# Two hypernetwork convolution layers: first weights by ScalarE, statistics merged in two steps, a normalization stage on VectorE, W2 and the hidden vectors loaded in other pieces

## The chip, the cores and the metric

The kernel runs on one core of a Trainium2 chip. A core has TensorE (matmuls and, beside them, weight loads), VectorE, ScalarE, GpSimd and SyncE; in the profile they are PE and PEld, DVE, ACT, POOL and SP. All transfers of this kernel are issued by SyncE, in program order. The metric is the device time of one execution in microseconds, and before and after are compared by the median of several executions.

## The reference

Two layers of the same form run one after the other on x, shaped (s, b, c, l) = (32, 32, 64, 256), float32. Each layer normalizes x by groups over l (32 groups of 8 positions; mean and variance over everything of one sample s that lies in the group: all b, all c, 8 l), convolves the result along l with weights that differ for every (b, l), adds a bias, and adds the input x back.

```python
h = jax.nn.relu(_ln(z @ W1 + b1, g1, be1))            # hidden vector of each (b, l)
w = (h @ W2 + b2).reshape(B, L, CI, CO, K)            # its own 64x64x3 weights
hb = jax.nn.relu(_ln(z @ Wb1 + bb1, gb1, beb1))
bias = (hb @ Wb2 + bb2).transpose(0, 2, 1)
xp = jnp.pad(x, ((0, 0), (0, 0), (0, 0), (pad, pad)))
x_uf = jnp.stack([xp[..., i:i + L] for i in range(K)], axis=-1)
out = jnp.einsum('sbilk,bliok->sbol', x_uf, w) + bias[None]
# layer: x = x + conv(_gn(x), ...)
```

The statistics of a layer need all of its x, so no product of a layer can start before the last piece of its input exists. The weights of a layer do not depend on x.

## The kernel before, in words

**Units.** u counts batches over both layers (64 in all; u = 32, written B, begins the second layer). v counts half-batches, 32 output channels each; v = 64, written NH * B, begins the second layer. For one v, TensorE makes the weights of all positions in 12 groups (`order`: 4 blocks of 8 output channels times 3 kinds), each one PSUM tile `pg` made from the hidden vector `hs[u]` and a piece of `w2` (lines 502 and 503, `make`). `take` adds b2 and puts the group into the SBUF tile `wall`: by VectorE for the kinds 0 and 1 and one half of kind 2 (line 514), by ScalarE for the other half of kind 2 (line 525), or wholly by ScalarE in eight or sixteen instructions if `scalar` is set. `products(v)` (line 548) then multiplies the normalized x in `xn` with `wall` in four groups of positions q, in two PSUM tiles `pc`; VectorE adds each group to the residual tile (line 558) and, in the first layer, takes its statistics (line 257).

**First phase** (`first_phase`). The whole of x is loaded in 16 blocks of 4 MiB (SyncE line 273, `load(q)`) into three places in turn, the last block into `xn`; block q + 3 is asked for after block q's statistics. VectorE takes the statistics of each block as it lands, into `first_parts`. Between them, spread evenly, runs the work on the hidden vectors of all 64 batches (class `Hidden`): z is loaded, TensorE, ScalarE, GpSimd and VectorE compute, and the hidden vectors and biases are stored to `hd` and `bd` in DRAM, one entry of `hd` for two batches. Also in SyncE's queue: four quarters of the first layer's W2 after the blocks 4 to 7, the hidden vectors of batches 0 and 1 after block 10 (line 124), and after block 14 batch 0's x (line 129) and two residuals (line 138). `first_weights` stands in front of block 14's statistics: GpSimd clears two strips of `wall`, and 9 of the first 12 weight groups are made and taken by ScalarE.

**From the statistics to the first product.** `batches` merges the parts of all batches into mean and variance (eight VectorE instructions, lines 368 to 375). `diagonals` takes the root on ScalarE and the reciprocal on VectorE, and lays mean and reciprocal root on diagonals: `gmean` by eight ScalarE instructions (402), `rstd` by one of VectorE (405). `spread` multiplies both with a matrix of ones on TensorE (419), so that every partition has them, and ScalarE copies them back (420). Then the last three weight groups are made and taken by VectorE, and VectorE normalizes batch 0 (`normalize_first`, 489) in three stages, each of four pieces with one subtraction and one multiplication. Meanwhile GpSimd adds the bias to the first residual (438).

**The train.** For every later v TensorE makes the first weight group of v, does the products of v - 1, and makes the other eleven. `after(v - 1)` stores the result, loads the residual of v + 1, the hidden vector of the next but one batch (when h = 1), stores pieces for the second layer (452), normalizes the next batch's half on GpSimd (`next_pairs`, 471, which then asks for the half of the batch after it, 131 in the second layer), and adds the next bias on GpSimd.

**Boundary.** After v = 63 there are statistics that only then are complete. The parts of all batches but the last were merged earlier (`batches(parts, B - 1)`); `last_batch` (382 to 392) merges the last in, `diagonals` follows, and after the fourth weight group of v = 64 `spread` and `normalize_first(B, nc.gpsimd)`, whose three stages run on GpSimd, then the loads of batch 33 and its normalization. A group q of products needs only some of the groups of positions: q = 0 is served by the first stage, q = 1 by the second as well, q = 2 and 3 by the third too.

The order on every engine and in SyncE's queue is the order of the program; nothing is rearranged.

## Time and profile before

| what | us |
|---|---|
| median of 9 runs | 4059.24 |
| lowest and highest of them | 4053.94, 4065.47 |
| the profiled execution's own time | 4065.47 |
| its span in the profile | 4063.5 |
| chain of work that ended last: TensorE's share | 87% |
| weights, PE lines 502 and 503, busy each | 2739.9, 2738.7 |
| products, PE line 548, busy | 976.7 |
| evictions of weights: DVE line 514, ACT line 525 | 1855.0, 1188.1 |

The profiled execution is the slowest of the nine. An "xN" behind an operation is a count; "<-" in brackets names what ended the idle time before an instruction. Matmuls overlap, so their busy times add up to more than the span. In the forty slices of the profile, TensorE is busy for six tenths and fewer in the first three slices (about 100 us each) and for nine tenths or more from then on; the granted TensorE clock stands at five to eight tenths in part of the first three slices and at nine tenths or more after them. The transfers move 334 and 335 GB/s in the first two slices, about half of that later.

### The profile page before, as it was taken

What the parts mean: (1) busy time and instruction counts of PE and PEld (TensorE: products, weight loads), DVE (VectorE), ACT (ScalarE), POOL (GpSimd) and SP (SyncE); (2) the same over time, 40 slices, a digit from 0 to 9 for tenths busy, and PEclk for the clock granted to TensorE, in tenths of its full rate; (3) what the DMA queues carried; (4) which work ended last, traced back from release to release, by engine and by line L of the source; (5) the groups of instructions that cost most, each with busy time, mean ns of one, the idle gap of its engine ahead of it and who ended that gap; (6) DMA issues with size and microseconds to landing.
All of it is one profiled execution on the core that took longest, in us unless ns stands there. A gap on an engine that the chain in (4) does not pass through costs nothing.

```text
span 4063.5 us, 194865 instructions
## 1 busy us (share of the span) xinstructions
PE 3867.3 (95%) x91064; PEld 3713.9 (91%) x91064; DVE 2601.7 (64%) x2934; ACT 1333.3 (33%) x4480; POOL 1944.5 (48%) x639
## 2 busy tenths in 40 slices
PE   6659999999999999999999999999999999999999
PEld 3349999999999999999988999999999999999998
DVE  7666666666666666666675556565656565656565
ACT  6542323333232323323222323232323233323232
POOL 5425553454345435534533645544554455445541
PEclk8579999999999999999999999999999999999999
DMA  8977777777777777777676545444544454445442
GB/s 334 335 259 194 198 171 188 184 184 186 181 190 176 190 171 187 185 180 187 166 193 178 171 139 171 130 161 139 171 130 161 142 168 140 159 146 156 141 147 88
DMA packets 655426, 718.59 MB, mean 177 GB/s; under 512 B 567380, under 2 KB 585112, under 8 KB 586136
## 3 DMA queue, kind: packets, MB, share of 16 engines
q1 hardware_dynamic: 654616, 706.13, 61.2%
q8 instruction: 711, 11.65, 1.2%
q14 instruction: 99, 0.81, 0.1%
HBM read 492.12 MB, written 213.91 MB: 174 GB/s over the span
## 4 chain that ended last, share of the span: by engine, by line
PE 87%; DVE 5%; DMA 3%; issue 2%; POOL 2%; ACT 1%; SPq 0%; DVEq 0%; POOLq 0%; ACTq 0%
PE pg L502 50%; PE pc L548 23%; PE pg L503 12%; DVE wall L514 2%; DVE parts L257 1%; DMA zt<-in_L_conv_z_dram 1%; DMA wall<-in_xs_dram 1%; DVE room L558 1%; PE p L185 1%; POOL xn L200 1%; POOL xn L489 1%; PE p L217 0%; DMA hd<-xn 0%; POOL xn L471 0%; DMA room<-in_xs_dram 0%
## 5 line engine op out<-in xcount | busy, mean ns | idle before, releaser
L502 PE MATMUL pg<-hT,w2t 128*64 128x128 f32 x24576 | 2739.9, 274 | 30.8 <-DVE wall L514 11.5
L503 PE MATMUL pg<-hT,w2t 128*64 128x128 f32 x24576 | 2738.7, 274 | 4.0 <-issue 3.4
L502 PEld LDWEIGHTS pg<-hT,w2t 128*64 128x64 f32 x24576 | 2685.6, 137 | 57.6 <-DVE wall L514 23.2
L503 PEld LDWEIGHTS pg<-hT,w2t 128*64 128x64 f32 x24576 | 2686.2, 137 | 9.0 <-issue 8.3
L514 DVE TENSOR_TENSOR wall<-pg,b 64x1024 f32<-64x1024 f32 x1527 | 1855.0, 1220 | 688.1 <-PE pg L503 684.7
L525 ACT ACTIVATE wall<-pg,b 64x128 f32<-64x128 f32 x4168 | 1188.1, 478 | 2605.3 <-DVE wall L514 2156.4
L471 POOL TENSOR_TENSOR xn<-room,gmean 128x2048 f32<-128x2048 f32 x124 | 572.6, 4618 | 1765.2 <-PE pc L548 1736.9
L548 PE MATMUL pc<-wall,xn 128*32 128x128 f32 (+2 forms) x40960 | 976.7, 253 | 59.3 <-issue 45.8
L548 PEld LDWEIGHTS pc<-wall,xn 128*32 128x32 f32 x40960 | 933.6, 111 | 106.8 <-issue 91.2
L558 DVE TENSOR_TENSOR room<-pc,room 128x512 f32<-128x512 f32 x512 | 353.9, 691 | 667.5 <-PE pc L548 601.8
L471 POOL TENSOR_TENSOR xn<-xn,rstd 128x2048 f32<-128x2048 f32 x124 | 655.3, 5285 | 9.7
L438 POOL TENSOR_TENSOR room<-room,bt 128x2048 f32<-128x2048 f32 x128 | 587.5, 4590 | 121.0 <-DMA bt<-bd 58.8
L257 DVE BATCH_NORM_STATS2 parts<-room 128x6 f32<-128x256 f32 (+1 forms) x592 | 241.7, 453 | 16.2 <-DMA room<-in_xs_dram 7.4
L200 POOL TENSOR_TENSOR xn<-xn 128x512 f32<-128x512 f32 (+2 forms) x192 | 103.8, 541 | 103.7 <-ACT xn L192 91.2
L257 DVE BATCH_NORM_STATS2 parts<-wall 128x6 f32<-128x512 f32 x160 | 97.6, 678 | 27.0 <-DMA wall<-in_xs_dram 27.0
L217 PEld LDWEIGHTS p<-ident,xn 128*128 128x128 f32 x256 | 45.4, 201 | 74.0 <-issue 62.1
L217 PE MATMUL p<-ident,xn 128*128 128x128 f32 x256 | 62.0, 410 | 44.4 <-DVE xn L209 39.7
L185 PE MATMUL p<-wc,zt 17*64 17x256 f32 x512 | 59.5, 602 | 28.2 <-DMA zt<-in_L_conv_z_dram 20.6
L185 PEld LDWEIGHTS p<-wc,zt 17*64 17x64 f32 x512 | 27.4, 206 | 59.4 <-issue 33.9
L219 ACT ACTIVATE xn<-p,vec 128x512 f32<-128x512 f32 x64 | 46.3, 773 | 21.3 <-PE p L217 21.3
L192 ACT ACTIVATE xn<-p 128x1024 f32<-128x1024 f32 x32 | 32.6, 1019 | 41.0 <-PE p L185 41.0
L213 ACT ACTIVATE xn<-p,var 128x128 f32<-128x128 f32 x128 | 36.4, 372 | 10.4 <-DVE xn L209 10.4
(59 smaller groups left out, 207.9 us busy)
## 6 DMA issues: line engine op xcount, KB each, us to landing
bt<-bd SPq DMA_DIRECT2D x512, 256.0 KB, 6.4
room<-in_xp_dram SPq DMA_DIRECT2D x64, 1024.0 KB, 9.7
room<-in_xs_dram SPq DMA_DIRECT2D x64, 1024.0 KB, 8.6
x<-room SPq DMA_DIRECT2D x64, 1024.0 KB, 5.3
x1p<-room SPq DMA_DIRECT2D x512, 128.0 KB, 6.7
room<-x1p SPq DMA_DIRECT2D x64, 1024.0 KB, 8.3
room<-x SPq DMA_DIRECT2D x64, 1024.0 KB, 8.3
out_dram<-room SPq DMA_DIRECT2D x64, 1024.0 KB, 4.9
```

The costliest lines, as they stand in the source:

```text
L185: nc.tensor.matmul(self.p1[r : r + C, 2 * j + k], self.zt[rows, k * P + r : k * P + r + C], self.t["wc"][rows], start=True, stop=True,)
L200: nc.gpsimd.tensor_tensor(to, self.sq[:, :, 0:w], self.sq[:, :, w : 2 * w], ALU.add)
L217: nc.tensor.transpose(p2[:, net, k * P : (k + 1) * P], hs[:, 2 * k + net, :], ident)
L257: nc.vector.bn_stats(out, y.rearrange("p o (a m) -> p o a m", a=2)[:, :, :, g * e : (g + 1) * e])
L438: nc.gpsimd.tensor_tensor(y, y, bts.pop(v), ALU.add)
L471: nc.gpsimd.tensor_tensor(o, i, b.to_broadcast(list(o.shape)), op)
L502: nc.tensor.matmul(pg[0:C, k, :], w[:, k0 * C : (k0 + 1) * C], h0, start=True, stop=True)
L503: nc.tensor.matmul(pg[C:P, k, :], w[:, k1 * C : (k1 + 1) * C], h1, start=True, stop=True)
L514: nc.vector.tensor_tensor(place(rows, a), pg[rows].rearrange("p o (t m) -> p t m o", t=NT), b2[n][rows, kind, None, None, o0 : o0 + OG].to ...
L525: nc.scalar.activation(place(rows, a)[:, :, :, k], pg[rows, k].rearrange("p (t m) -> p t m", t=NT), AF.Identity, bias=b2[n][rows, kind, o0 ...
L548: nc.tensor.matmul(pc[t * S : (t + 1) * S, n0 - q * EB : n1 - q * EB, :], xn[:, u % 2, t * MT + p + 1, :], wall[:, t, a : a + (n1 - n0) * CH],
L558: nc.vector.tensor_tensor(part, pc.rearrange("p (m a) o -> p o a m", a=2), part, ALU.add)
```

## The change

1. In the first phase all 12 weight groups of v = 0 are made in `first_weights` and taken by ScalarE; none is left behind the spread.
2. The first layer's W2 is loaded in two halves: the first after block 7 (line 112's quarters after blocks 4 to 7 before), the second after block 14, between batch 0's x and the residuals.
3. The first layer's statistics are merged in two steps: `batches` over all batches but the last two, in front of the last block's statistics, then `last_batches`, which is `last_batch` made general, over these two.
4. `normalize_first` does one stage a call. In the first layer all three still run on VectorE. At the boundary stages 1 and 2 stay on GpSimd after the fourth weight group, and stage 3 is put on VectorE after the twelfth; the loads of batch 33 and its normalization follow stage 3.
5. Hidden vectors are loaded for two batches at a time, into tiles of twice the size: batches 0 to 3 after block 10, and then two batches after every odd one.
6. `spread` takes the number of groups for one matmul, separately for `gmean` and `rstd`, counted within each half.

```diff
+    hs = {}
...
-    def load_hidden(u):
-        h = hp.tile([P, 2, M], FP, tag="hT", name="hT")
-        nc.sync.dma_start(out=h, in_=hd[u // 2][u % 2].rearrange("p (a m) -> p a m", a=2))
-        return h
+    def load_hidden(i):
+
+        h = hp.tile([P, 2, 2, M], FP, tag="hT", name="hT")
+        nc.sync.dma_start(
+            out=h.rearrange("p b a m -> p b (a m)"), in_=hd[i].rearrange("b p f -> p b f")
+        )
+        for b in range(2):
+            hs[2 * i + b] = h[:, b]
...
                 if i == (NQ - 2) * SQ:
                     first_weights()
+                if i == (NQ - 1) * SQ:
+                    batches(first_parts, B - SV // NH)
...
-                if q + 8 in range(NQ - 4, NQ):
-                    o0 = (q + 12 - NQ) * C // 4
-                    load_w2(0, o0, o0 + C // 4)
+                if q == NQ - 9:
+                    load_w2(0, 0, CH)
                 if q == NQ - 6:
-                    for u in range(2):
-                        hs[u] = load_hidden(u)
+                    for j in range(2):
+                        load_hidden(j)
                 if q == NQ - 2:
 
                     for k in range(2):
                         load_pairs(0, k)
+                    load_w2(0, CH, C)
                     for v in range(2):
                         load_residual(v)
...
-    def last_batch():
-
-        n = 2 * NH * B
-        means, squares, shape = halves(parts, B - 1, B)
+    def last_batches(parts, u0):
+
+        n = 2 * parts.shape[3] * B
+        means, squares, shape = halves(parts, u0, B)
...
-        nc.vector.tensor_scalar(v, v, 1.0 - 1.0 / B, None, ALU.mult)
+        nc.vector.tensor_scalar(v, v, u0 / B, None, ALU.mult)
...
-    def spread(*how):
-
-        for to, (n, w) in zip((gmean, rstd), how):
+    def spread(steps, w):
+
+        for to, step in zip((gmean, rstd), steps):
             ps = ps_g.tile([P, G, S], FP, tag="pg", name="spread")
-            for k in range(n):
-                gs = slice(k * G // n, (k + 1) * G // n)
+            for g in [b + k for b in (0, G // 2) for k in range(0, G // 2, step)]:
+                gs = slice(g, min(g + step, g // (G // 2) * G // 2 + G // 2))
...
-        def normalize_first(u, eng):
+        def normalize_first(u, stage, eng):
...
-            for g0, g1 in ((-1, 3), (3, 5), (5, 7)):
-                for t in range(NT):
...
-            if u + 1 < U:
+            g0, g1 = ((-1, 3), (3, 5), (5, 7))[stage]
+            for t in range(NT):
...
+            if stage == 2:
                 for k in range(2):
                     load_pairs(u + 1, k)
+                next_pairs(u + 1, 0)
...
-            if h == 1 and u + 2 < U:
-                hs[u + 2] = load_hidden(u + 2)
+            if h == 1 and u % 2 == 1 and u + 3 < U:
+                load_hidden((u + 3) // 2)
             if v + 1 == NH * B:
                 store_pairs(v, range(8))
-                last_batch()
+                last_batches(parts, B - 1)
...
-            for k in range(9):
+            for k in range(len(order)):
                 weights(0, k, True)
...
-        batches(first_parts, B)
+        last_batches(first_parts, B - SV // NH)
         diagonals()
-        spread((2, P), (2, P))
-        for k in range(9, len(order)):
-            weights(0, k)
-        normalize_first(0, nc.vector)
-        next_pairs(1, 0)
+        spread((16, 8), P)
+        for stage in range(3):
+            normalize_first(0, stage, nc.vector)
...
-                    spread((8, C), (4, C))
-                    normalize_first(B, nc.gpsimd)
-                    next_pairs(B + 1, 0)
+                    spread((4, 6), C)
+                    for stage in range(2):
+                        normalize_first(B, stage, nc.gpsimd)
+            if v == NH * B:
+                normalize_first(B, 2, nc.vector)
```

## The prediction

> **What bounds the kernel now.** I read the busy shares first, then the chain that ended last.
>
> ```profile
> PE 3867.3 (95%) x91064; PEld 3713.9 (91%) x91064; DVE 2601.7 (64%) x2934; ACT 1333.3 (33%) x4480; POOL 1944.5 (48%) x639
> ...
> PE 87%; DVE 5%; DMA 3%; issue 2%; POOL 2%; ACT 1%; SPq 0%; DVEq 0%; POOLq 0%; ACTq 0%
> ```
>
> TensorE sets the time, except in two places: the first 305 us, where x is streamed in for the statistics, and the layer boundary near 2200 us. Whatever either place loses is added to the end, because behind it comes an even train of half-batches that TensorE bounds. So I look only at what ends last in those two. First the VectorE timeline of the start; the bracket is the idle time before an instruction and what ended it.
>
> ```profile
> 232.65 9.59 DVE L257 BATCH_NORM_STATS2 parts<-wall 128x6 f32<-128x512 f32 x16 [5.18 <-DMA wall<-in_xs_dram]
> 248.39 9.59 DVE L257 BATCH_NORM_STATS2 parts<-room 128x6 f32<-128x512 f32 x16 [6.16 <-DMA room<-in_xs_dram]
> 263.97 9.59 DVE L257 BATCH_NORM_STATS2 parts<-xn 128x6 f32<-128x512 f32 x16 [5.99 <-DMA xn<-in_xs_dram]
> 273.59 0.83 DVE L368 TENSOR_REDUCE prep<-parts 128x8 f32<-128x512 f32 x1
> ...
> 277.93 0.17 DVE L375 SCALAR_TENSOR_TENSOR prep<-prep 128x8 f32<-128x8 f32 x1
> ...
> 289.05 1.22 DVE L514 TENSOR_TENSOR wall<-pg,b 64x1024 f32<-64x1024 f32 x1 [9.12 <-PE pg L503]
> ...
> 293.68 0.55 DVE L489 TENSOR_TENSOR xn<-room,gmean 128x384 f32<-128x384 f32 x1
> ...
> 304.94 0.56 DVE L489 TENSOR_TENSOR xn<-xn,rstd 128x384 f32<-128x384 f32 x1
> 305.41 0.68 DVE L558 TENSOR_TENSOR room<-pc,room 128x512 f32<-128x512 f32 x1
> ```
>
> Each of the last blocks is awaited; the transfers set the pace up to 273.6. Then everything is serial: merge, diagonals and spread (to 288.15, the end of ScalarE's copy of rstd), three weight evictions, normalization, first residual add. The SyncE timeline shows what the transfers carry: loads of x blocks (L273) and a quarter of W2 (L112).
>
> ```profile
> 88.35 0.48 SPq L273 DMA_DIRECT2D wall<-in_xs_dram  x1
> ...
> 104.73 0.55 SPq L273 DMA_DIRECT2D wall<-in_xs_dram  x1
> 105.34 0.43 SPq L112 DMA_DIRECT2D w2t<-in_L_conv_W_dram  x1
> ...
> 126.62 0.55 SPq L273 DMA_DIRECT2D room<-in_xs_dram  x1
> ```
>
> A block takes 16.4 us without a quarter behind it, 21.9 with one. Then the boundary, GpSimd and VectorE:
>
> ```profile
> 2220.44 0.86 POOL L489 TENSOR_TENSOR xn<-room,gmean 128x256 f32<-128x256 f32 x1
> ...
> 2226.54 0.99 POOL L489 TENSOR_TENSOR xn<-xn,rstd 128x384 f32<-128x384 f32 x1
> 2231.72 4.58 POOL L471 TENSOR_TENSOR xn<-room,gmean 128x2048 f32<-128x2048 f32 x1 [4.18 <-DMA room<-x1p]
> ...
> 2253.01 4.63 POOL L438 TENSOR_TENSOR room<-room,bt 128x2048 f32<-128x2048 f32 x1
> ```
>
> ```profile
> 2228.96 0.69 DVE L558 TENSOR_TENSOR room<-pc,room 128x512 f32<-128x512 f32 x1 [6.49 <-PE pc L548]
> ...
> 2257.68 1.29 DVE L558 TENSOR_TENSOR room<-pc,room 128x512 f32<-128x512 f32 x2 [4.97 <-POOL room L438]
> ```
>
> The third normalization stage on GpSimd (2220.44 to 2227.53) holds up the third group of products, and then everything behind it on GpSimd: batch 33's load and normalization, then the bias add that the next half awaits.
>
> **1. W2 split in two, the second half behind the last block.** Block loads go out at 57.10, 73.82, 88.35, 104.73, 126.62, 146.11, 165.91, 185.50, 201.81, 218.34 and 233.31. The four gaps with a quarter of W2 average 20.2 us, the six others 15.9, so the 6 MiB cost 4 x 4.3 = 17.1. Half of it leaves the stretch before the last block: -8.6. The first two hidden loads are together 0.25 MiB larger at the same place: +0.7 at 17.1/6 us per MiB. Net -7.9. Bounds: 0, if the blocks waited for something else, and -8.7 (3.15 MB at the stretch's 335 GB/s, less 0.7). I take -7.9, since the gaps measure just this. On SP the half now stands ahead of the loads of residuals 0 and 1 and bias 0. The bytes up to the bias are the same (0.25 MiB more), so bias 0 lands about when it did, 279.2 + 0.7, and GpSimd adds it from 280 to 285. The half itself is wanted by weights of the next half at about 277, and lands some 24 us after the last block's load goes out at 243.5 (9.4 MB at 395 GB/s, the mean of 255 to 275 us in the windows), at 267.
>
> **2. Early merge.** The eight merge instructions (273.59 to 278.10, 4.5 us) move before the last block, into VectorE's 5.99 us of idle there; in their place stand the eleven of the last-batch merge, which the boundary shows at 2192.04 to 2193.88, 1.8 us. -2.7. If that idle time were gone, the 4.2 us of merging would be back, for a loss of 1.5 instead.
>
> **3. All twelve weight groups on ScalarE.** It now takes
>
> ```profile
> 238.17 26.05 ACT L525 ACTIVATE wall<-pg,b 64x128 f32<-64x128 f32 x96 [11.85 <-DVE parts L257]
> ```
>
> 0.271 us each; 128 take 34.7, to 272.9. The root on ScalarE is wanted at 273.56 + 1.8 = 275.4; both times move up with step 1, so 2.5 us of cover remain. What leaves the path is the wait for TensorE and VectorE's three evictions between the rstd copy's end and the normalization. The first subtraction needs gmean alone (copied by 285.71) and goes ahead; the first multiplication starts at 288.2 instead of 294.33: -6.1. The spread's matmuls keep their total of columns; two more instructions in the first layer and a few at the boundary lie at 0.3 us or less.
>
> **4. What the earlier normalization meets.** It would run from 276.4 to 287.6 and now shares that time with the bias add on GpSimd, which ran before it until now. Does a VectorE operation with two SBUF operands slow GpSimd? Nearest row: of the 128 bias adds,
>
> ```profile
> L438 POOL TENSOR_TENSOR room<-room,bt x128: 4532/4582/4856, 279.4 to 4014.0; 128x2048 f32<-128x2048 f32 x128
> ```
>
> the longest is the first; only it lies beside such an operation (rstd<-ident,prep, 278.70 to 279.92). It lost 0.27 us in 0.49 of overlap, 55%, and VectorE lost nothing (1.22, as in the boundary). At 55% the add would do 45% of 7.5 us beside the normalization, 3.4 of 4.6, and end at 288.8: +1.2 on the first residual add. Bounds 0 and +4.6 (no overlap at all). The Trainium skill says more ("SBUF — State Buffer", section "SBUF: two separate sides"): the port pair of VectorE and GpSimd is an exclusive lock, held for a whole instruction, also against VectorE operations with two SBUF inputs. The row is a loss in that direction, though of half the overlap; by the rule this step would be +4.6 and the next -2.5, the sum -14.6 rather than -20.0.
>
> **5. Boundary: stage three on VectorE.** Its eight operations took 301.97 to 305.50 in the first layer, 3.5 us; VectorE is free for them at 2217.56, so they end at 2221.1. SP has issued its stores by 2212.7 and POOL has only stages one and two, so the loads of batch 33 (two, 1 MiB each) and all behind go out once both engines have read x. Without hindrance that is 2220.8 instead of 2226.49: -5.7, and the chain to the bias add of 2253.01 shifts as a whole; products alone would gain 6.6. With the 55% of step 4, stage two ends at 2222.7 and its last subtraction at 2222.0: -4.5. Fully serial: -2.5. VectorE reading x with this layout's stride is not shown here; at GpSimd's price for the stage, 7.1 us, it would end at 2224.7, 2.9 earlier than now, and with full hindrance on top nothing is left. I take -4.5, since the row of step 4 is the nearest, bounds 0 and -5.7.
>
> **6. Hidden loads by two batches.** In the train 30 loads of 256 KiB take the place of 62 of 128 KiB. Bytes are the same, no wait of TensorE for them stands in the train, and each is issued at least a batch ahead of its use: 0. What queues behind one on SP are the pair stores and the next bias load (rival C).
>
> **Sum:** -7.9 - 2.7 - 6.1 + 1.2 - 4.5 = -20.0. The profiled execution took 4065.47 (span 4063.5), the highest of nine runs; against the median 4059.24 the forecast is 4039.2.
>
> **Rivals.**
> A: the last block comes no earlier. For it: the last load waits for the bias stores (bd<-xn) that read its buffer, not for bytes. Against: those stores lie in the same queue behind the block before. Then -12.1: 4047.
> B: the two engines exclude each other fully, -14.6: 4044.6. For it the row of step 4; against it, half the overlap was free.
> C, slower: the double hidden load stalls the train. It stands on SP ahead of the pair stores and the bias load, 30 times. From the first residual add of each half I read periods of 28.4 to 30.4 us, mean 29.78 in the first layer where a hidden load was issued and 29.50 where not; so up to 0.28 for 128 KiB. It decides from 0.94 us more per pair of batches, 28 us in all; at 1 us the time is 4069. Against it: twice the load half as often is zero, and the second layer shows 28.65 with and 29.24 without.
> D: the gain is given back early in the train, where one period is 33.6 us with TensorE idle for 3.2 ("issue") at 336.5 while transfers crowd in; packed tighter, two or three more such stalls eat 10 us: 4051 to 4055.
>
> **Numbers.** Forecast 0.62, A 0.14, B 0.10, C 0.08, D 0.06. About 0.2%, 8 us, is what a measurement here can tell from no change: faster is below 4051. The forecast, A and B lie there, less 0.04 for A and B with an unlucky median (the nine runs span 11.5): 0.82; same 0.10 from D and that; slower 0.08. The range goes from all terms at their good bounds (-8.7 - 2.7 - 6.1 - 5.7 = -23.2, and half the runs' spread, 6, below it: 4030) to A with 6 on top, 4053.
>
> **What would show it.** Right: last block's statistics start near 256 instead of 263.97, with about 6 us of idle before the early merge; rstd copied near 277.5; ScalarE's 128 in one train of 35 us that ends before the root; first residual add near 290; at the boundary the third group's idle of 6.49 nearly gone and the bias add of 2253 about 4.5 earlier relative to the residual add before it; periods unchanged. Wrong: the last block at 264 again (A); the bias add or VectorE's operations lengthened by their whole overlap (B); periods after odd batches longer by a microsecond (C); ScalarE still evicting when the root is due.

## The result and the profile after

The changed kernel takes 4042.93 us (median of 9 runs, 4033.95 to 4046.8) against 4060.6 for the kernel before (29 runs on the same chip): a ratio of 0.9955, with a 95% interval of 0.9947 to 0.9964, or 17.7 us. The forecast was 4039.2 (20.0 below the 4059.24 then known of before) and the range 4030 to 4053.

The busy shares and the chain that ended last, on the page of after, say that TensorE's work hardly changed (3859.3 us busy against 3867.3); its shares rose because the span shrank.

```profile
PE 3859.3 (96%) x91076; PEld 3709.3 (92%) x91076; DVE 2610.3 (65%) x2950; ACT 1339.6 (33%) x4504; POOL 1938.0 (48%) x631
...
PE 89%; DVE 5%; DMA 3%; issue 2%; POOL 1%; ACT 1%; SPq 0%; DVEq 0%; ACTq 0%; POOLq 0%
```

**Where the time went.** The residual adds of VectorE are milestones: the first of half-batch 0, and the first of half-batches 63 and 66, on either side of the boundary. Both kernels were also profiled once more on another chip, so there are two pairs (us):

| | before | after | change | before again | after again | change |
|---|---|---|---|---|---|---|
| start to first residual add | 305.4 | 293.8 | -11.6 | 304.7 | 292.3 | -12.4 |
| half-batch 0 to 63 | 1876.0 | 1870.4 | -5.6 | 1876.3 | 1879.0 | +2.7 |
| 63 to 66, the boundary | 104.0 | 99.4 | -4.6 | 103.8 | 99.2 | -4.6 |
| 66 to the end of the span | 1778.1 | 1776.8 | -1.3 | 1777.5 | 1772.8 | -4.7 |
| span | 4063.5 | 4040.4 | -23.1 | 4062.3 | 4043.4 | -18.9 |

The start and the boundary repeat to a microsecond and give 16.2 and 17.0 us together. The first layer's train gains 5.6 us in one pair and loses 2.7 in the other, and in after alone it differs by 8.6 us between two profiles. So nearly all of the medians' 17.7 us is the start and the boundary; what the trains gain or lose here is no larger than their own scatter.

**The start.** The VectorE timeline of after, the bracket being the idle time before an instruction and what ended it:

```profile
223.19 9.58 DVE L263 BATCH_NORM_STATS2 parts<-wall 128x6 f32<-128x512 f32 x16 [3.56 <-DMA wall<-in_xs_dram]
239.99 9.59 DVE L263 BATCH_NORM_STATS2 parts<-room 128x6 f32<-128x512 f32 x16 [7.22 <-DMA room<-in_xs_dram]
249.61 0.79 DVE L376 TENSOR_REDUCE prep<-parts 128x8 f32<-128x480 f32 x1
...
257.46 9.59 DVE L263 BATCH_NORM_STATS2 parts<-xn 128x6 f32<-128x512 f32 x16 [3.33 <-DMA xn<-in_xs_dram]
...
268.75 0.17 DVE L400 TENSOR_TENSOR prep<-prep 128x8 f32<-128x8 f32 x1
...
278.55 0.56 DVE L496 TENSOR_TENSOR xn<-xn,rstd 128x384 f32<-128x384 f32 x1 [1.44 <-ACT rstd L428]
...
280.35 0.68 DVE L496 TENSOR_TENSOR xn<-room,gmean 128x512 f32<-128x512 f32 x1
281.07 4.87 DVE L496 TENSOR_TENSOR xn<-xn,rstd 128x512 f32<-128x512 f32 x1
285.86 0.68 DVE L496 TENSOR_TENSOR xn<-room,gmean 128x512 f32<-128x512 f32 x1
...
293.80 0.68 DVE L566 TENSOR_TENSOR room<-pc,room 128x512 f32<-128x512 f32 x1
```

The last three blocks arrive 9.5, 8.4 and 6.5 us earlier than before. In the second pair it is 8.0 us for the last one (263.26 to 255.22). The big merge begins at 249.61, in front of the last block, and 3.33 us of idle time are left behind it, so the last block is still awaited. Behind the last block the short merge ends at 268.92. The first multiplication starts at 278.55 instead of 294.33; in before it came 6.18 us after the end of ScalarE's copy of `rstd`, here 0.03. The copy in the ScalarE timeline of before, then in that of after:

```profile
287.14 1.01 ACT L420 COPY rstd<-spread 128x1024 f32<-128x1024 f32 x1 [1.43 <-PE spread L419]
```

```profile
277.51 1.01 ACT L428 COPY rstd<-spread 128x1024 f32<-128x1024 f32 x1 [0.99 <-PE spread L427]
```

But the line at 281.07 took 4.87 us, where its neighbours of the same shape took 0.69. The GpSimd timeline of after shows what lay beside it, the first bias add:

```profile
280.45 4.93 POOL L445 TENSOR_TENSOR room<-room,bt 128x2048 f32<-128x2048 f32 x1 [12.97 <-DMA bt<-bd]
```

It was busy from 280.45 to 285.38, and the multiplication that started at 281.07 ended at 285.94, 0.56 behind it. The ScalarE timeline of after shows that the twelve weight groups never were in the way: the train ends at 263.4, and the root comes at 268.95, after 5.59 us of idle time.

```profile
228.71 34.65 ACT L533 ACTIVATE wall<-pg,b 64x128 f32<-64x128 f32 x128 [10.07 <-DVE parts L263]
...
268.95 0.30 ACT L405 ACTIVATE prep<-prep,eps 128x8 f32<-128x8 f32 x1 [5.59 <-DVE prep L400]
```

**The boundary.** The VectorE timeline of after: stage three, and the residual adds behind it.

```profile
2197.41 1.02 DVE L496 TENSOR_TENSOR xn<-room,gmean 128x256 f32<-128x256 f32 x1
...
2199.17 1.23 DVE L496 TENSOR_TENSOR xn<-room,gmean 128x256 f32<-128x256 f32 x1
...
2201.14 0.62 DVE L496 TENSOR_TENSOR xn<-room,gmean 128x256 f32<-128x256 f32 x1
...
2202.97 0.56 DVE L496 TENSOR_TENSOR xn<-xn,rstd 128x384 f32<-128x384 f32 x1
...
2207.68 0.69 DVE L566 TENSOR_TENSOR room<-pc,room 128x512 f32<-128x512 f32 x1 [2.95 <-PE pc L556]
...
2233.88 0.69 DVE L566 TENSOR_TENSOR room<-pc,room 128x512 f32<-128x512 f32 x1 [2.52 <-POOL room L445]
```

The GpSimd and the SyncE timeline of after, from the first operation of stage one to the bias add that the next half-batch awaits, and the loads of batch 33 that lie between:

```profile
2183.09 1.20 POOL L496 TENSOR_TENSOR xn<-room,gmean 128x384 f32<-128x384 f32 x1 [20.04 <-ACT gmean L428]
...
2200.06 0.88 POOL L496 TENSOR_TENSOR xn<-xn,rstd 128x256 f32<-128x256 f32 x1
2208.13 4.57 POOL L478 TENSOR_TENSOR xn<-room,gmean 128x2048 f32<-128x2048 f32 x1 [7.19 <-DMA room<-x1p]
...
2229.16 4.68 POOL L445 TENSOR_TENSOR room<-room,bt 128x2048 f32<-128x2048 f32 x1
```

```profile
2203.01 10.04 SPq L137 DMA_DIRECT2D room<-x1p  x3
```

The loads go out when VectorE's last subtraction has read x, 19.9 us after the first operation of stage one. In before the same distance is 23.3. Its GpSimd and its SyncE timeline:

```profile
2203.16 1.19 POOL L489 TENSOR_TENSOR xn<-room,gmean 128x384 f32<-128x384 f32 x1 [23.20 <-ACT gmean L420]
```

```profile
2226.49 10.15 SPq L131 DMA_DIRECT2D room<-x1p  x3
```

The residual add of the third group waits 2.95 us for its products, where it waited 6.49. The chain from the loads to the bias add of 2229.16 moved as a whole (26.15 us long, 26.52 in before).

### The profile page after: what moved, and what is told of

Read it like the earlier page. It is cut to its first block, busy times and chain, and to the rows that moved or that the text cites. A ratio compares the mean times of both kernels' runs of the same rounds, so it can differ in the third digit from the quotient of the medians.

```text
span 4040.4 us, 194819 instructions
## 1 busy us (share of the span) xinstructions
PE 3859.3 (96%) x91076; PEld 3709.3 (92%) x91076; DVE 2610.3 (65%) x2950; ACT 1339.6 (33%) x4504; POOL 1938.0 (48%) x631
## 3 DMA queue, kind: packets, MB, share of 16 engines
q8 instruction: 711, 11.65, 1.2%
## 4 chain that ended last, share of the span: by engine, by line
PE 89%; DVE 5%; DMA 3%; issue 2%; POOL 1%; ACT 1%; SPq 0%; DVEq 0%; ACTq 0%; POOLq 0%
PE pg L510 51%; PE pc L556 24%; PE pg L511 13%; DVE wall L522 2%; DVE parts L263 1%; DMA hd<-xn 1%; DVE room L566 1%; POOL xn L206 1%; DMA wall<-in_xs_dram 1%; DMA w2t<-in_L_conv_W_dram 1%; PE p L223 0%; PE p L191 0%; DMA room<-in_xs_dram 0%; DMA xn<-in_xs_dram 0%; DMA zt<-in_L_conv_z_dram 0%
## 5 line engine op out<-in xcount | busy, mean ns | idle before, releaser
L445 POOL TENSOR_TENSOR room<-room,bt 128x2048 f32<-128x2048 f32 x128 | 587.6, 4591 | 127.5 <-DMA bt<-bd 49.9
L206 POOL TENSOR_TENSOR xn<-xn 128x512 f32<-128x512 f32 (+2 forms) x192 | 103.8, 541 | 96.4 <-ACT xn L198 83.8
L191 PEld LDWEIGHTS p<-wc,zt 17*64 17x64 f32 x512 | 27.0, 204 | 54.0 <-issue 35.1
```

What stands on the lines that cost most here:

```text
L191: nc.tensor.matmul(self.p1[r : r + C, 2 * j + k], self.zt[rows, k * P + r : k * P + r + C], self.t["wc"][rows], start=True, stop=True,)
L206: nc.gpsimd.tensor_tensor(to, self.sq[:, :, 0:w], self.sq[:, :, w : 2 * w], ALU.add)
L445: nc.gpsimd.tensor_tensor(y, y, bts.pop(v), ALU.add)
```

## The experiments

The theory was the prediction's sum with one term changed: the first bias add and VectorE's normalization exclude each other. The rivals were that they share (55%, the prediction's value), that the gain comes from other parts of the change than those I named, and, for the trains, that the paired hidden loads cost or save something. All ratios are to the kernel before on the same chip (4066.3, 4066.2 and 4069.1 us on the three occasions).

### The first bias add left out

```diff
-        next_bias(0)
+        bts.pop(0)
+        load_bias(1)
```

> The changed kernel without GpSimd's bias add to the first residual (the first half-batch's bias is left out of the result; the next bias load goes out at once instead of after that add). Theory of mutual exclusion: in the changed kernel one VectorE multiplication of the first normalization took 4.87 us instead of 0.69 because GpSimd's add (280.45 to 285.38) held what both need; without the add no operation of that normalization is longer than 0.75 us, it runs 11.1 us from its first multiplication to the first residual add instead of 15.25, and the first residual add starts 4.2 us earlier against the end of the spread. Rival: the long operation comes from the transfers that land at that time (second half of W2, residuals, bias); then it stays between 3 and 5 us, somewhere in that normalization. In the total 4 us less than the changed kernel by the first theory, 0 by the second; a few us of spread between runs lie on top.

4051.98 us, 0.9959 (0.9945 to 0.9973). The VectorE timeline of this kernel:

```profile
278.56 0.56 DVE L496 TENSOR_TENSOR xn<-xn,rstd 128x384 f32<-128x384 f32 x1 [2.26 <-ACT rstd L428]
...
281.08 0.69 DVE L496 TENSOR_TENSOR xn<-xn,rstd 128x512 f32<-128x512 f32 x1
...
289.64 0.68 DVE L566 TENSOR_TENSOR room<-pc,room 128x512 f32<-128x512 f32 x1
```

The multiplication that took 4.87 us takes 0.69. From the first multiplication to the first residual add it is 11.08 us, to the hundredth what it was in before, and 15.25 in after. So the two do not share: one VectorE instruction waited for the whole of GpSimd's, for 4.2 us. The residual add is earlier; the total is not measurably lower than that of after on another chip (0.9962, below). In the profile the first layer's train takes 1886.6 us, against 1870.4 and 1879.0 in the two profiles of after, and TensorE's waits for "issue", that is for nothing that the profile shows, are 35.1 us in its products, against 25.7 and 29.0. That led to the last two groups of experiments.

### W2 in quarters, as before

```diff
-                if q == NQ - 9:
-                    load_w2(0, 0, CH)
+                if q + 8 in range(NQ - 4, NQ):
+                    o0 = (q + 12 - NQ) * C // 4
+                    load_w2(0, o0, o0 + C // 4)
...
-                    load_w2(0, CH, C)
```

> The changed kernel with W2's four quarters back behind blocks 4 to 7 and no second half behind block 14. If W2 delays the blocks by its bytes, the last block's statistics start 6 to 8 us later than in the changed kernel (257.46), near 264. Then the bias add of GpSimd, whose bytes are the same, ends (about 285) before or just as the normalization starts (about 283 to 284), the two no longer collide for more than 2 us, and the first residual add comes only 2.5 to 4 us later than in the changed kernel (293.80): the W2 move is worth 2.5 to 4 us. If the collision has nothing to do with when the bias lands, the first residual add comes the full 6 to 8 us later. If the blocks do not wait for bytes, nothing moves.

4049.92 us, 0.9962 (0.9948 to 0.9976). The VectorE and the GpSimd timeline of this kernel:

```profile
262.90 9.59 DVE L263 BATCH_NORM_STATS2 parts<-xn 128x6 f32<-128x512 f32 x16 [1.46 <-DMA xn<-in_xs_dram]
...
281.68 2.57 DVE L496 TENSOR_TENSOR xn<-room,gmean 128x384 f32<-128x384 f32 x1 [5.50 <-ACT gmean L428]
...
295.43 0.68 DVE L566 TENSOR_TENSOR room<-pc,room 128x512 f32<-128x512 f32 x1
```

```profile
279.31 4.52 POOL L445 TENSOR_TENSOR room<-room,bt 128x2048 f32<-128x2048 f32 x1 [6.39 <-DMA bt<-bd]
```

The last block comes 5.4 us later than in after (7.7 later than in its repeat), about the size of step 1. But the first residual add is only 1.6 us later (295.43 against 293.80; 3.1 against the repeat of after), where 2.5 to 4 had been expected. With the block later, the bias add ends at 283.83 beside the first subtraction, in a time in which VectorE would have waited for `rstd` anyway: in after 1.44 us of such a wait stand before the first multiplication, in the kernel above 2.26, here none. The collision costs 1.0 us there (the copy of `rstd` ends at 283.32, the first multiplication starts at 284.35) and not 4.2. So of what the halves of W2 gain, about half, 3.2 of 5.4 or 7.7 us, goes back to the collision that they bring about. In the total this cannot be told apart from after.

### Stage three on GpSimd, as before

```diff
-                    for stage in range(2):
+                    for stage in range(3):
                         normalize_first(B, stage, nc.gpsimd)
-            if v == NH * B:
-                normalize_first(B, 2, nc.vector)
```

> The changed kernel with the third normalization stage of the boundary back on GpSimd, after the fourth weight group, and batch 33's loads behind it there. If that stage is worth what the two traces show, the loads of batch 33 go out 23.3 us after the first operation of stage one instead of 19.9, the residual add that waits for the bias comes 3.5 to 4 us later, and the total is 3 to 5 us above the changed kernel. If the difference of the traces at the boundary came from TensorE's stall in front of it (2.8 us, put down to issue, in the profile of before only), the total is within 1 us of the changed kernel.

4053.02 us, 0.9964 (0.9952 to 0.9977). The boundary takes 103.1 us from the add of half-batch 63 to that of 66, against 99.4 and 99.2 in the two profiles of after. The GpSimd and the SyncE timeline of this kernel:

```profile
2191.26 1.21 POOL L496 TENSOR_TENSOR xn<-room,gmean 128x384 f32<-128x384 f32 x1 [21.58 <-ACT gmean L428]
```

```profile
2214.69 10.04 SPq L137 DMA_DIRECT2D room<-x1p  x3
```

The loads of batch 33 go out 23.4 us after the first operation of stage one. In before, its repeat and the kernel with paired loads alone (below) it is 23.3, 23.4 and 23.4; in all profiles read with the stage on VectorE it is 19.9 (after, its repeat, and five experiments). So the stage is worth 3.5 us at this place, and by these profiles 3.7 to 3.9 at the boundary as a whole, which scatters more (102.0 and 102.5 in two kernels below that have the stage on VectorE). The other 0.7 to 0.9 us of the boundary's 4.6 are not the stage's. The total does not resolve it: 3 to 5 us more than after had been expected, and the ratios are the same.

### Both kernels again

> The kernel before, profiled on the chip of the runs beside it. On another chip of this study its median was 4066.27 against 4060.6. If that difference is the chip's, in the wait of TensorE for its own instructions, its profile shows more than the 26 us of idle put down to issue in the first layer's train (380 to 2100 us); if the train's stalls belong to the kernel, 26 again.

> The changed kernel again, on the chip of the runs beside it, to compare them with: ratio to before 0.9955 (0.9947 to 0.9964) if the gain doesn't depend on the chip; first residual add near 293.8, idle put down to issue in the first layer's train near 30 us.

After: 4048.94 us, 0.9962 (0.995 to 0.9974). Before, one run with a profile: 4064.36. These are the pair in the table above. The collision repeats: 4.87 us for the multiplication at 279.57. TensorE's waits for "issue" in the first layer's products are 26.8 us in this before and 25.2 in the first one, 29.0 in this after and 25.7 in the first one.

### Hidden vectors one by one, in the changed kernel

```diff
-            if h == 1 and u % 2 == 1 and u + 3 < U:
-                load_hidden((u + 3) // 2)
+            if h == 1 and u + 2 < U:
+                load_hidden(u + 2)
```

and, in a second kernel, also the pieces of `spread` as they were in before:

```diff
-        spread((16, 8), P)
+        spread((16, 16), P)
...
-                    spread((4, 6), C)
+                    spread((4, 8), C)
```

> The changed kernel with hidden vectors loaded one batch at a time as before. By the prediction's step the loads cost nothing either way: total within 2 us of the changed kernel, mean periods of the train unchanged (29.43 and 29.71 us in the first layer, 29.18 and 28.66 in the second, for even and odd halves). Rival: the train's own gain, 5.6 us between the first residual add and the boundary in the two traces, comes from there being half as many of these loads; then the total is 4 to 6 us above the changed kernel and the periods of the first layer are back at 29.50 and 29.78.

> The changed kernel with hidden vectors loaded one batch at a time, and with the spread's matmuls cut as in the kernel before, so that TensorE's stream of instructions in the train has the length that it has before. The run with single loads alone stood at 0.9995 of before, with 44 us of stalls that each end 1.3 to 1.6 us after a 16 KiB transfer of instructions, against 26 in the two traces at hand. Theory of single loads: these transfers of 128 KiB make the stalls; then the ratio is 0.9985 to 1.001 again. Theory of alignment: which matmul stands at the edge of a 16 KiB piece decides; then the train is as before and the ratio is 0.994 to 0.997.

The first takes 4065.31 us, 0.9995 (0.9986 to 1.0004): all of the gain is gone. The second takes 4057.73, 0.9978 (0.997 to 0.9987): with six matmuls of the program fewer in `spread` (12 matmuls and 12 weight loads in the profile), some half of it is back. Neither time lies where one of its theories had put it. Neither edit touches the start (first residual add at 293.3 and 293.5) or the distance of 19.9 us to the loads of batch 33. What grows is the first layer's train, 1892.6 and 1881.0 us from half-batch 0 to 63 against 1870.4 and 1879.0, and the boundary by 2 to 3 us, with TensorE's waits for nothing that the profile shows ("issue"; the columns are us in total, times, longest), in the view of waits from 380 to 2100 us, first of the one kernel, then of the other:

```profile
PE pc L552 <- issue: 41.3, 62, 1.3
```

```profile
PE pc L552 <- issue: 30.4, 46, 1.3
```

### Hidden vectors in pairs, in the kernel before

```diff
-            if h == 1 and u + 2 < U:
-                hs[u + 2] = load_hidden(u + 2)
+            if h == 1 and u % 2 == 1 and u + 3 < U:
+                load_hidden((u + 3) // 2)
```

> The kernel before with one part of the change alone: hidden vectors loaded for two batches at a time. By the prediction's step this costs and gains nothing: ratio 1.000 within 0.0015. By the theory that the double loads carry most of the gain: ratio 0.996 to 0.9975, periods of the first layer's train shorter by 0.2 us on average, and stalls for instructions fewer than in the kernel before beside it.

4079.01 us, 1.0036 (1.0022 to 1.005). Neither expectation holds. The same edit that looks worth 0.3 to 0.4% in the changed kernel (0.9955 and 0.9962 against 0.9995) costs 0.36% in the kernel before. So the loads as such are neither good nor bad. In the profile (the fastest of its ten runs) the first layer's train is shorter than in before, 1863.5 against 1876.0, and the second longer, 1797.5 against 1778.1. The waits for "issue" go the same ways. The view of waits of this kernel, from 380 to 2100 us and from 2290 to 4030; then the repeat of before, in the same windows:

```profile
PE pc L553 <- issue: 15.8, 35, 0.9
...
PE pc L553 <- issue: 26.1, 56, 0.9
```

```profile
PE pc L548 <- issue: 26.8, 46, 1.3
...
PE pc L548 <- issue: 11.2, 25, 1.0
```

**What TensorE waits for there.** The page's table of DMA queues has a queue that no instruction of the kernel issues to:

```profile
q8 instruction: 711, 11.65, 1.2%
```

711 transfers of 11.65 MB are 16 KiB each, and TensorE has 91,076 matmuls and as many weight loads; at 64 bytes each (16 KiB by 256) they make 11.66 MB. So this queue brings TensorE's instructions, in pieces of 256. I set the ends of these transfers beside TensorE's idle times of over 0.3 us without a releaser in the trains: TensorE starts again 1.27 to 1.56 us after such a transfer has ended (10th to 90th percentile). A half-batch is 384 matmuls for weights, 320 for products and as many weight loads, 1408 instructions or 5.5 pieces. So two half-batches are 11 pieces, the edges stand at nearly the same place in every second half-batch, and an edit that adds or drops instructions ahead of a train moves them all at once. "Nearly", because the traces of TensorE also hold semaphore instructions, in the train one for each hidden load: 158 in the changed kernel with single loads and 126 with pairs, 155 and 123 in the kernel before. So the edits to the hidden loads change TensorE's stream too, by 32 instructions spread over the trains. The next kernels test whether the place of the edges matters.

The Trainium skill ("Runtime: NRT & Kernel Launch", section "Instruction fetch mechanics") states the same size, blocks of 16 KiB or 256 instructions, fetched while the engine works, and calls the cost of a boundary mostly hidden. The size agrees with the 711 transfers; whether the cost is hidden is what the next kernels measure.

### Three quarters of the second half of W2 behind the first bias, and idle instructions

The first of these kernels tries to get the first bias in before the collision: only the first 8 output channels of the second half of W2 stay in front of the residuals, the rest follows the first bias. The three others are this one with 64, 128 or 192 TensorE instructions more ahead of the train, products of `ones` and `ident` that nothing uses, in `first_weights`.

```diff
-                    load_w2(0, CH, C)
+                    load_w2(0, CH, CH + OG)
...
         load_bias(0)
+        load_w2(0, CH + OG, C)
```

```diff
             for k in range(len(order)):
                 weights(0, k, True)
+            pad = ps_c.tile([P, EB, CH], FP, tag="pc", name="pad")
+            for k in range(N // 4):
+                nc.tensor.matmul(pad[:, 0], ones, ident[:, 0:CH], start=True, stop=True)
```

> The changed kernel with the second half of W2 cut once more: its first 8 channels stay in front of the residuals, the other 24 are asked for after the first bias load. Theory of collision: the bias then lands about 6 us earlier (2.4 MB at 395 GB/s), GpSimd's add (280 to 285 in the changed kernel) ends before or within 1 us of the normalization's first multiplication, no VectorE operation there is longer than 2 us, the last block's load no longer shares its time with 2.4 MB of W2 (1 to 2 us earlier), and the first residual add starts at 287 to 290 instead of 293.8; the total is 4 to 6 us below the changed kernel, if the train stalls for instructions as there. Rival: TensorE waits for the late 24 channels; then the weights of the second half-batch come late by more than 2 us and the gain is gone.

4048.53 us, 0.9958 (0.9945 to 0.997), no other than after. The bias add began only 1.7 to 3.2 us earlier than in the two profiles of after and still lies beside the normalization; the first residual add comes at 292.7, not at 287 to 290. The VectorE and the GpSimd timeline of this kernel:

```profile
278.24 3.91 DVE L496 TENSOR_TENSOR xn<-xn,rstd 128x384 f32<-128x384 f32 x1 [1.43 <-ACT rstd L428]
```

```profile
277.22 4.52 POOL L445 TENSOR_TENSOR room<-room,bt 128x2048 f32<-128x2048 f32 x1 [10.04 <-DMA bt<-bd]
```

This time the first multiplication is the one that waits, until 0.41 behind the add's end at 281.74. So 3.3 us of the 4.2 remain.

> The run with W2 cut once more, with 16 matmuls more (64 instructions of TensorE) at the end of the first weight groups, where TensorE is idle; their product is used nowhere. Theory of alignment: TensorE's instructions come in pieces of 16 KiB, 256 instructions, two half-batches are 2816 instructions or exactly 11 pieces, so a shift by 64 moves every edge in the train by the same 64 instructions; idle time put down to issue in the train changes by several us against the run without pad, and the total with it, by 5 to 20 us either way for at least two of the three pads. Rival: the stalls come from the transfers alone (their number and size); then all four runs stay within 4 us and the stalls within 5 us of each other.

> As with 64, with 32 matmuls more (128 instructions, half a piece). By the theory of alignment the largest difference to the run without pad: since one half-batch is 5.5 pieces, a shift by half a piece exchanges the roles of even and odd half-batches; stalls that stood in the fourth group of products of even halves and in the third of odd ones stand there the other way round, and the sum over the train changes little in each layer if both kinds are alike. By the rival nothing changes.

> As with 64, with 48 matmuls more (192 instructions, three quarters of a piece). By the theory of alignment its train is that of the run with 64 with even and odd halves exchanged, so its stalls and total are near that run's and not near those of the runs with 0 and 128. By the rival all four runs are alike within 4 us.

The added instructions themselves are hidden: the first residual add is at 288.2, 293.0 and 293.1 us, against 292.7 without them. Yet the kernels take 4095.66, 4111.29 and 4124.56 us: 1.0073 (1.006 to 1.0087), 1.0108 (1.0094 to 1.0122) and 1.014 (1.0126 to 1.0154), that is 47, 63 and 76 us more than the same kernel without. The view of waits from 380 to 2100 us, of the kernels with 64 and with 128, and of that with 192 in the same window and from 2290 to 4110:

```profile
PE pc L556 <- issue: 52.4, 88, 1.5
```

```profile
PE pc L556 <- issue: 66.5, 89, 1.4
```

```profile
PE pc L556 <- issue: 34.7, 65, 1.4
...
PE pc L556 <- issue: 35.7, 82, 0.9
PE pg L511 <- issue: 14.0, 18, 1.5
```

Without them it is 35.0 us in the first layer and 9.7 in the second. So a shift of the instruction stream, with the program of the trains unchanged, goes with 47 to 76 us, about three to four times the gain under study. The four kernels issue the same data transfers in the same order, so those alone, the rival here, can't be the reason. (The unused products also take one of the two `pc` tiles in turn; that is the same in all three and can't explain the 29 us between 64 and 192.) What I had expected of the sizes failed: the loss does not come back to nothing at 128, and 192 is not like 64; with 192 it sits mainly in the second layer (1842.4 us from half-batch 66 to the end, against 1778.5 without).

**What the traces settle.** I numbered all instructions of TensorE in each trace from the first, weight loads, matmuls and semaphore instructions alike, and looked at each number's place within its 256. All of TensorE's waits for "issue" (idle times over 0.15 us) in the trains of all fourteen profiles, 1554 of them, stand at place 193 or 194. If the semaphore instructions are left out of the count, they spread over 16 to 31 places. So these waits are waits at the edges of the pieces, and the edits to the hidden loads do move the edges. Then I added up the time from one matmul's start to the next over both trains (from half-batch 1 to 63 and from 66 to 30 us before the end), apart for matmuls at the edges (672 to 675) and for all others (some 86,000), in us:

| kernel | at the edges, first and second layer | elsewhere |
|---|---|---|
| before; again | 70.6 + 47.4; 73.7 + 46.5 | 3477.7; 3475.5 |
| after; again | 69.1 + 47.2; 75.5 + 44.1 | 3472.9; 3473.8 |
| single hidden loads; and old spread | 91.0 + 46.8; 73.8 + 47.8 | 3473.3; 3476.4 |
| before with paired loads | 56.0 + 65.8 | 3481.6 |
| W2 cut once more | 79.6 + 49.4 | 3474.9 |
| the same with 64; 128; 192 more | 100.1 + 55.7; 121.5 + 49.9; 76.1 + 109.2 | 3486.1; 3475.8; 3486.0 |

What the trains lose to the shifts stands at the edges: 27, 42 and 56 us of the 38, 43 and 67 by which the trains of these profiles grow. Of the other 11 with 64 and with 192, nearly 8 are more waiting for other engines, in the main for VectorE's evictions (line 522); why was not followed up. At an edge of after the next matmul starts 0.17 us after the last on average, elsewhere 0.04; that makes some 90 us of the whole. The skill's "mostly hidden" fits the number of edges, since only 92 of the 673 in after show a wait of over 0.15 us; it does not fit the price, which a shift of the stream changes by 1 to 2% of the kernel. Why one place of the edges costs more than another stays open.

## Why the prediction was right, step by step

The sign, the size and the range held: 4042.9 against 4039.2, with the gain in the two places named, and none elsewhere that repeats. Steps 1 to 3 were right as a mechanism, step 4 was not, and that the total came so near is in part luck. Steps 2 and 3 were not undone one by one; their sizes are read from the two pairs of traces.

1. **W2 in halves, -7.9: -6.5** in the profile of after (263.97 to 257.46), -8.0 in the second pair, and 5.4 to 7.7 where it was undone. The gaps between the blocks were a good price; rival A (no earlier) fell. That part of it would be given back through step 4 I did not see.
2. **Early merge, -2.7: -2.67.** From the end of the last block's statistics to the end of the merge it was 4.51 us (273.59 to 278.10) and is 1.84 (267.08 to 268.92); in the second pair 4.52 and 1.83.
3. **Twelve groups on ScalarE, -6.1: -6.15.** The first multiplication starts 15.78 us earlier, of which 9.63 are the earlier copy of `rstd` (288.15 to 278.52); in the second pair this step is -6.14. ScalarE was through 5.6 us before the root, where I had counted 2.5: its train began 9.5 us earlier (238.17 to 228.71), more than the last block did.
4. **Bias add beside the normalization, +1.2: +4.2.** This is the term that failed most, by 3.0 us, and the wrong engine waited in it: the step slowed GpSimd's add and left VectorE's operations as they were, but in after the add lost some 0.35 us (4.93 against its usual 4.58) and VectorE 4.2. (The step's window of 276.4 to 287.6 also lies 0.6 us earlier than the sum's own terms put the normalization, 293.68 - 16.7 = 277.0; that is small beside the miss.) The step said "At 55% the add would do 45% of 7.5 us beside the normalization". The runs show no sharing: 15.25 us with the add, 11.08 without. My row, an add of 4.856 with "0.27 us in 0.49 of overlap", was over-read: from the end of VectorE's instruction at 279.92 that add ran 4.37 us more, and in after, where it waited for VectorE's until 281.03, it ran 4.35 more. Both fit an add that begins its work when VectorE's instruction ends. The Trainium skill ("SBUF — State Buffer", section "SBUF: two separate sides") had said so: an exclusive lock for a whole instruction, also against VectorE operations with two SBUF inputs. The profile of after agrees, with 4.87 us for an operation of 0.69, and the rule's +4.6 was the nearer estimate.
5. **Stage three on VectorE, -4.5: -3.4 and -3.5 to the loads in the two pairs, -3.5 where it was undone.** Between the forecast and the fully serial -2.5. VectorE took 6.1 us for the stage (2197.41 to 2203.53), not 3.5: 3.8 for the first four operations, beside GpSimd's last ones (1.02, 0.72, 1.23, 0.80), and 2.4 for the other four, alone. Of these, the subtractions that read x in this layout took 0.62 and 0.80 instead of 0.42 and 0.55 in the first layer, which the prediction had left as unknown. GpSimd lost some 0.5 us. That the loss stays small although the two exclude each other fits operations that are short on both engines, each waiting for one of the other's at a time; no run tested that by itself.
6. **Hidden loads in pairs, 0.** No wait for them appears, so rival C fell in its own terms. But the edit takes 32 semaphore instructions out of TensorE's stream and so moves the edges of its pieces, and what that does to the trains depends on what else is in the kernel (0.9995 without the pairs in the changed kernel, 1.0036 with them in the kernel before). "Periods unchanged" held by luck: all parts of the change together left the time at the edges as it was, 118.1 and 120.2 us in before, 116.2 and 119.6 in after. Rival D (stalls early in the train) named the right kind of wait, "issue", but not its place or cause: the period that it named, from half-batch 1 to 2, was 33.6 and 32.4 us in the two profiles of before and 30.6 and 32.8 in those of after.

At the start the measured sizes add up to -6.5 - 2.7 - 6.15 + 4.2 = -11.15 in the first pair and -8.0 - 2.7 - 6.15 + 4.2 = -12.65 in the second; the copy of `rstd` after the merge came 0.45 us sooner in the one and 0.3 later in the other, which makes the -11.6 and -12.4 of the table. The boundary gave -4.6 twice, of which 3.4 and 3.5 are step 5's. So the terms missed by 3.0 us in step 4 and 1.0 in step 5, both too hopeful, and by 1.4 or -0.1 in step 1; that the medians still differ by 17.7, against 20.0 forecast, owes about 1 us at the boundary to something that no step named, and the rest is within the trains' scatter. Rival B had the right mechanism in step 4 and too high a price in step 5; its 4044.6 is even nearer to the result than the forecast's 4039.2, so the total does not choose between them. The profile does, for B at the start and against it at the boundary.

## What to carry to other kernels

Price a chain by the engines beside it, too: work that is pulled forward meets what used to run before it, and a GpSimd operation of 4.5 us beside short VectorE ones with two SBUF inputs costs its whole length, while beside a wait it costs nothing. Read a gain of some tenths of a per cent in the place where it arises (distance between two milestones, in two profiles), and not from the total, for in a stream of 180,000 TensorE instructions a shift by 64 of them cost more than the change gained. Undo a part in both kernels before you call it good or bad: the paired loads had opposite signs.

## What the runs showed that I had not expected

- 64, 128 or 192 unused TensorE instructions ahead of an otherwise equal train cost 47, 63 and 76 us of 4050, 1.2 to 1.9%, and most of it stands at one place of every 256 instructions.
- A VectorE subtraction of 256 float32 elements a partition took 0.62 us where it read x in the second layer's layout, beside nothing on GpSimd, and 0.42 in the first layer's; with 384 elements 0.80 and 0.55.
- The load of the last x block took 14.6 us from its issue to its statistics in after and 12.6 in before, which is more than the 1.4 us by which step 1 fell short. The second half of W2 stands behind it in the queue, but that alone is not the reason: with that half behind it the load took 12.5 us in the repeat of after and 12.4 to 14.1 in four experiments (no first add, stage three on GpSimd, both with single loads), without it 12.5 to 12.6 in four profiles. What made the difference stays open.
